# Two convolution layers with deformable sampling: hat loads in a running list, tails begun at the last unit that writes their rows, and the last tile row's branches reversed

## The chip, the cores and the metric

The kernel runs on 1 core of one Trainium2 chip. The metric is device time in microseconds (us) of one launch. The kernel before took 6643.4 us, the median of 3 runs (6639.72 to 6648.73).

## What is computed

The input x has shape (2, 256, 128, 128): two images of 256 channels and 128 x 128 pixels, in float32. Two layers are added to it in turn. Cut to what matters:

```python
x = x + layer0(group_norm(x))
x = x + conv3x3(group_norm(x), ternary_weights) + bias

def layer0(x):                                  # d = 1, 9, 12
    for d in dilations:
        off = conv3x3(x, w_off[d], dilation=d)  # 18 planes: (dy, dx) of 9 taps
        y = sum over 9 taps of w_def[c, tap] * bilinear(x, pixel + tap * d + off)
        x_d = gelu(channel_norm(y))
    out = channel_norm(x_1 + x_9 + x_12 + conv1x1(x))
    h = gelu(out @ w1 + b1) @ w2 + b2           # 256 -> 512 -> 256 per pixel
    return channel_norm(h + out)
```

## The kernel before

Three stages follow each other. The first computes moments and offsets and writes two things to DRAM: `tables`, x with the pixel as the row, and `hats`, the bilinear weights of each tap as two factors, one for the row and one for the column. The second, `sample_near` (L1257), samples and does the rest of layer 0. The third is the 3x3 convolution of layer 1. Between stages stands a branch that all engines pass.

Sampling goes by *units*, in the list `units` (L1262): image b, tile row Rt of 66 (two pixel rows each), branch br of 3 (dilations 1, 9, 12), in this order of nesting. A unit has up to three *taps* ky (L1310), those whose rows fall within the image. Near the top and the bottom of an image units have two taps or one: every unit of the first tile row and of the last has one, and branches 1 and 2 have two in many of the rows next to them.

For each tap `load_hats` (L1313) loads two tiles, hy and hx, of 288 KB each (half that where one row is valid), into three buffers of each name, from SP's queue. `build` (L1333) multiplies them on DVE into the matrix A, of which there are two, used in turn. `load_tiles` (L1291) loads the 11 xs tiles of a tile row, 96 KB each, into 18 buffers, also from SP's queue. `sample` (L1422 on) multiplies A with xs on PE for each of two halves of the channels, into four PSUM banks pm; ACT copies these to ev (L1460, L1468), of which there are three, and `accumulate` adds ev to the ring of the branch on DVE (L1409); the first tap of a new row is written by ACT (L1391). A ring holds 8, 24 or 32 rows of a branch. `prepare(u)` (L1477) builds all taps of unit u and then calls `load_hats(u + 1)`; unit u prepares unit u + 2 ahead of its second half's sums. After unit 1 `lacking` (L1498) does a block of DVE work on the few pixels that lie outside.

Four rows of a branch make a *group*, of which an image has 32. When its rows are complete a *tail* is begun for it (`branch`, L1156): it turns the rows (PE, tp), copies them (ACT), takes moments (DVE L1097 to L1102, POOL L1103 and L1104), scales and applies gelu (ACT L1111). Branch 0 stores the result in g12d, branch 1 loads that as `other`, adds it and stores the sum, and branch 2 loads the sum, adds it and goes on: the 1x1 convolution (PE, pc), norm, zc, the two layers of the MLP (PE hp L890 and h L1133), norm, zc, and the store in x1d. Tails are generators. `tail.begin` (L1504) queues one, first in, first out, ready 7 advances later (LAG), and with at least 2 advances (GAP) from one start to the next; `tail.advance` moves the running ones by a step. A unit of sampling advances them four times, and `accumulate` advances them as often as is needed before it writes a ring row whose old group has not been read yet (L1388). After the last unit a loop advances until all are done (L1508): the drain. The order of compute instructions is thus written out by hand (`pin`), and that of the DMAs on a queue follows a scheduler.

Which unit begins a group is worked out at L1264 to L1274: the first unit of the branch after which all rows of the group lie below what later tile rows reach, or the last tile row for what is left. `spot` (L1276) prepares the corrections of a branch 0 group on DVE and needs `count`, loaded at L1489.

Of the kernel before, what the change touches and what calls it, by code (L numbers as in the profile page):

```python
# [25 lines left out]
R = 4  # L26
NG = R * W
RC = 16
DILS = (1, 9, 12)
# [10 lines left out]
REACH = 2  # L40
RI, CI = 2, 12
TR, TC = RI + 2 * REACH, CI + 2 * REACH
NT = -(-(W + 2 * REACH) // CI)
# [7 lines left out]
BRS = (0, 1, 2)  # L51
# [20 lines left out]
def conv_preact_kernel(ctx: ExitStack, tc: tile.TileContext, t: dict, out: bass.AP):  # L72
    nc = tc.nc
    x = t["x"]
    NB, _, H, _ = x.shape
    HW = H * W
    NGRP = H // R
    NR = (H + 2 * REACH) // RI
# [629 lines left out]
    with ExitStack() as actx:  # L708
# [24 lines left out]
        for b in range(NB):  # L733
            stats = ap.tile([P, KC, NGRP, 6], F32, name=f"stats1_{b}", tag=f"stats1_{b}")
            for c in range(KC):
                for g0 in range(0, NGRP, XT):
                    xt = ap.tile([P, XT * NG], F32, name="xt", tag="xt", bufs=3)
# [97 lines left out]
    class Tail:  # L835
# [4 lines left out]
        def __init__(self, pool, psum, pin):  # L840
            self.pool, self.psum, self.pin = pool, psum, pin
            self.spots, self.extra = {}, None
            self.waiting, self.running = deque(), []
            self.now = self.last = self.norms = self.banks = 0
            self.read = set()

        def begin(self, chain, wait):
            self.waiting.append([self.now + wait, chain, 0, 1, False])
# [122 lines left out]
        def branch(self, b, br, g, y):  # L971

            pin = self.pin
            cols = slice(g * NG, (g + 1) * NG)
            gv = g12d[b].rearrange("(k p) f -> p k f", p=P)[:, :, cols]
            z = []
            yield from self.normalised(z, y, (b, br, g))
            v = z[0]
            for c in range(KC):
                pin(  # L980
                    nc.scalar.activation(
                        v[:, c, :], z[1 + c], AF.Gelu,
                        scale=bw[:, br, c : c + 1], bias=bb[:, br, c : c + 1],
                    )
                )
            if br == 0:
                yield 2
                nc.sync.dma_start(gv, v)
                return
            yield 1, 1 + br  # L990
            other = self.tile("other")
            nc.sync.dma_start(other, gv)
            if br == 1:
                yield 2
                pin(nc.vector.tensor_tensor(v, v, other, ALU.add))
                yield 2
                nc.sync.dma_start(gv, v)
                return
            xn = self.tile("xn")
            nc.sync.dma_start(xn, x[b].rearrange("(k p) h w -> p k (h w)", p=P)[:, :, cols])  # L1000
            yield 4
            for c in range(KC):
                pin(
                    nc.scalar.activation(
                        xn[:, c, :], xn[:, c, :], AF.Identity, bias=negmean[b][:, c : c + 1]
                    )
                )
            yield 1
            yield from self.finish(b, g, v, other, xn)
# [75 lines left out]
    class PixelTail(Tail):  # L1085
# [70 lines left out]
        def branch(self, b, br, g, y):  # L1156
# [16 lines left out]
            if br == 0:  # L1173
                yield 2
                nc.sync.dma_start(gv, vf)
                return
            other = self.tile("other")
            of = other.rearrange("p k n -> p (k n)")
            nc.sync.dma_start(of, gv)
            if br == 1:  # L1180
                yield 2
                pin(nc.vector.tensor_tensor(vf, vf, of, ALU.add))
                yield 2
                nc.sync.dma_start(gv, vf)
                return
            yield 1, 3
            xn = self.tile("xn")
# [69 lines left out]
    def sample_near(pool, psum, k):  # L1257
# [1 line left out]
        pin = tc.keep_in_program_order  # L1259
        count = pool.tile([P, NG], F32, name="count")  # L1260
        tail = PixelTail(pool, psum, pin)
        units = [(b, Rt, br) for b in range(NB) for Rt in range(NR) for br in BRS]  # L1262
        xts, hbs, owners, begun = {}, {}, {}, set()
        done = {(b, br): 0 for b in range(NB) for br in BRS}  # L1264
        begins, order = {}, []
        for u, (b, Rt, br) in enumerate(units):
            begins[u] = []
            while done[b, br] < NGRP and (
                Rt == NR - 1
                or (done[b, br] + 1) * R - 1 < (Rt + 1) * RI - REACH - DILS[br]  # L1270
            ):
                begins[u].append((b, br, done[b, br]))
                done[b, br] += 1
            order += [(wb, wg) for wb, wbr, wg in begins[u] if wbr == 0]  # L1274

        def spot(n):  # L1276

            if n >= len(order):
                return
            b, g = order[n]  # L1280
            S = pool.tile([P, NG], BF16, name="S", tag="S", bufs=5)
            if n >= 5:
                assert (order[n - 5][0], 2, order[n - 5][1]) in tail.read
            pin(
                nc.vector.tensor_scalar(
                    S, count, float((b * NGRP + g) * NG), ids, ALU.add, ALU.is_equal
                )
            )
            tail.spots[order[n]] = S

        def load_tiles(b, Rt):  # L1291

            xts[b, Rt] = []
            for T in range(NT):
                xt = pool.tile([PX, C], F32, name="xs", tag="xs", bufs=18)
                src = bass.AP(
                    table[b].tensor,
                    table[b].offset + (Rt * RI * WT + T * CI) * C,
                    [[C, TC], [WT * C, TR], [1, C]],
                )  # L1300
                nc.sync.dma_start(xt, src)
                xts[b, Rt].append(xt)

        def valid(Rt, br, ky):

            s0 = Rt * RI - REACH - ky * DILS[br]
            i0, i1 = max(0, -s0), min(RI, H - s0)
            return (i0, i1) if i0 < i1 else None

        def taps(u):  # L1310
            return [ky for ky in (-1, 0, 1) if valid(units[u][1], units[u][2], ky)]

        def load_hats(u):  # L1313
            b, Rt, br = units[u]
            for ky in taps(u):
                i0, i1 = valid(Rt, br, ky)
                hq = hats[b][br * 3 + ky + 1]
                y0 = Rt * RI - REACH - ky * DILS[br] + i0
                hy = pool.tile([PX, RI, 3, W], F32, name="hy", tag="hy", bufs=3)
                hx = pool.tile([PX, RI, 3, W], F32, name="hx", tag="hx", bufs=3)  # L1320
                pitch = HY * 3 * W
                for h, first, dims in (
                    (hy, 0, [[0, TC], [pitch, TR]]),
                    (hx, TR, [[pitch, TC], [0, TR]]),
                ):
                    src = hq[first, y0]
                    nc.sync.dma_start(
                        h[:, i0:i1].rearrange("p i t w -> p (i t w)"),
                        bass.AP(src.tensor, src.offset, dims + [[1, (i1 - i0) * 3 * W]]),
                    )  # L1330
                hbs[u, ky] = hy, hx

        def build(u, ky):  # L1333

            b, Rt, br = units[u]
            dil = DILS[br]
            i0, i1 = valid(Rt, br, ky)
            hy, hx = hbs.pop((u, ky))

            Af = k["A"][u % len(k["A"])].rearrange("p t i w -> p (t i w)")  # L1340
            dst = bass.AP(
                Af.tensor,
                Af.offset + ((ky + 1) * 3 * RI + i0) * WA + AO + REACH - dil,
                [list(Af.ap[0]), [RI * WA + dil, 3], [WA, i1 - i0], [1, W]],
            )
            pin(
                nc.vector.tensor_tensor(  # L1347
                    dst,
                    hy[:, i0:i1].rearrange("p i t w -> p t i w"),
                    hx[:, i0:i1].rearrange("p i t w -> p t i w"),  # L1350
                    ALU.mult,
                )
            )
# [123 lines left out]
        def prepare(u):  # L1477

            if u < len(units):
                for ky in taps(u):  # L1480
                    build(u, ky)
                if u + 1 < len(units):
                    load_hats(u + 1)

        load_hats(0)
        load_tiles(*units[0][0:2])
        prepare(0)
        prepare(1)
# [1 line left out]
        begun_groups = 0  # L1490
        spot(0)
        for u, (b, Rt, br) in enumerate(units):
            if br == BRS[0] and u + len(BRS) < len(units):
                load_tiles(*units[u + len(BRS)][0:2])
            for c in range(KC):
                sample(u, c)
            if u == 1:
                tail.extra = lacking(pool, tail.tile, miss, pin)  # L1498

            for what in begins[u]:  # L1500
                _, _, g = what
                r0 = g * R % RINGS[br]
                ring = k["rings"][br][:, :, r0 : r0 + R, :].rearrange("p k r w -> p k (r w)")
                tail.begin(tail.branch(b, br, g, ring), LAG)  # L1504
                if br == 0:
                    begun_groups += 1
                    spot(begun_groups)
# [462 lines left out]
```

## Time and profile before

| | |
|---|---|
| median of 3 runs | 6643.4 us |
| profiled execution | 6654.54 us |
| its span, first to last instruction | 6652.5 us |
| mean granted TensorE clock | 0.971 |
| busy: PE, PE weight loads, DVE, ACT, POOL | 6295.0, 5006.0, 5907.6, 4194.8, 687.1 us |
| first stage, sampling, last stage (from its windows) | 0 to about 916, to about 5858, to the end |
| chain that ended last: PE, DVE, DMA, ACT, issue | 54%, 28%, 8%, 6%, 3% |
| sampling matmuls, pm L1448 | 17424, 344 ns each |
| DVE waiting for hx at the build, L1347 | 100.2 us in 59 waits |

The page lists for every engine its busy time, the chain that ended last, groups of instructions by line, and DMA issues. Times within the execution count from the start of its span. PE is the matmul row, PEld its weight loads, which overlap it; SPq is SP's DMA queue. A matmul of float32 stands as two records. In brackets behind an instruction stands how long its engine was idle before it, and who ended that.

### The profile page before, as it was taken

How to read it: one execution, taken by the hardware profiler on the slowest of the kernel's cores; microseconds unless marked ns; L12 is line 12 of the kernel's file. 1: busy time of each engine (PE TensorE's matmuls, PEld its weight loads, DVE VectorE, ACT ScalarE, POOL GpSimd, SP SyncE). 2: the span in 40 equal slices, each digit the busy share in tenths (PEclk: the TensorE clock that was granted, in tenths of full speed). 3: DMA queues.
4: the chain of work that ended last, by engine and by line, in shares of the span. 5: the costliest groups of instructions: out<-in, count | busy, mean ns of one | idle time of the engine just before them, and what ended most of it. 6: DMA issues, size and time to landing. Idle time of an engine off the chain costs nothing.

```text
span 6652.5 us, 100588 instructions
## 1 busy us (share of the span) xinstructions
PE 6295.0 (95%) x32242; PEld 5006.0 (75%) x32242; DVE 5907.6 (89%) x13772; ACT 4194.8 (63%) x8690; POOL 687.1 (10%) x665
## 2 busy tenths in 40 slices
PE   5899978999999999999999999999999999989999
PEld 3455558888888888888888888888888888734444
DVE  7766657999999999999878999999999999689996
ACT  1344436677777777777676777777777777554442
POOL 0000000111111111111110111111111111200000
PEclk9999978999999999999999999999999999989999
DMA  8976657877887777877667877778777787343332
GB/s 285 281 211 196 201 158 208 227 220 218 222 224 217 219 215 222 226 220 210 189 192 199 226 221 218 216 221 229 224 217 220 218 222 207 121 163 132 135 141 90
DMA packets 635794, 1360.48 MB, mean 205 GB/s; under 512 B 109592, under 2 KB 290344, under 8 KB 618736
## 3 DMA queue, kind: packets, MB, share of 16 engines
q1 hardware_dynamic: 617328, 1318.97, 68.8%
q10 hardware_dynamic: 17408, 33.56, 1.6%
q8 instruction: 261, 4.28, 0.3%
q14 instruction: 285, 2.33, 0.1%
q0 software_dynamic: 512, 1.34, 0.1%
HBM read 1087.10 MB, written 266.47 MB: 203 GB/s over the span
## 4 chain that ended last, share of the span: by engine, by line
PE 54%; DVE 28%; DMA 8%; ACT 6%; issue 3%; SPq 1%; POOL 0%; DVEq 0%; ACTq 0%; POOLq 0%
PE pm L1448 23%; DVE ring L1409 12%; PE hp L890 6%; PE pc L1789 6%; PE h L1133 5%; PE pz L364 4%; DVE A L1347 4%; DMA hx<-hats 3%; ACT ev L1460 3%; PE pc L1133 2%; DMA xa<-in_x 2%; ACT v L1111 2%; PE ph L463 2%; PE tp L905 1%; DVE st L1097 1%
## 5 line engine op out<-in xcount | busy, mean ns | idle before, releaser
L1448 PE MATMUL pm<-A,xs 96*128 96x216 f32 (+2 forms) x17424 | 3258.3, 344 | 180.3 <-ACT ev L1460 44.4
L1448 PEld LDWEIGHTS pm<-A,xs 96*128 96x128 f32 x17424 | 3058.0, 195 | 380.0 <-ACT ev L1460 124.2
L1409 DVE SCALAR_TENSOR_TENSOR ring<-ev,defw,ring 128x256 f32<-128x256 f32 (+4 forms) x6372 | 2481.2, 451 | 98.1 <-ACT ev L1460 52.1
L1460 ACT COPY ev<-pm 128x432 f32<-128x432 f32 (+4 forms) x4488 | 1991.9, 483 | 883.2 <-PE pm L1448 702.4
L1347 DVE TENSOR_TENSOR A<-hy,hx 96x768 f32<-96x768 f32 (+1 forms) x1124 | 1010.3, 945 | 180.3 <-DMA hx<-hats 100.2
L1103 POOL TENSOR_TENSOR rs<-rs,mhalf 128x4 f32<-128x4 f32 x320 | 472.5, 1477 | 4223.5 <-DVE rs L1102 3672.0
L1789 PE MATMUL pc<-cring,signs 128*128 128x512 bf16 x3456 | 758.2, 383 | 17.0 <-ACT cring L1706 7.4
L1111 ACT ACTIVATE v<-v,rs 128x256 f32<-128x256 f32 x1280 | 694.2, 594 | 17.0 <-POOL rs L1104 16.8
L1789 PEld LDWEIGHTS <-signs 128*128 128x128 bf16 x3456 | 339.7, 98 | 434.8 <-issue 28.0
L890 PE MATMUL hp<-S,w 128*128 128x512 f32 x1024 | 500.5, 614 | 0.8 <-ACT S L1213 0.8
L364 PE MATMUL pz<-wz,xa 128*128 128x486 f32 x1024 | 463.5, 580 | 28.1 <-DVE zr L371 28.0
L1097 DVE BATCH_NORM_STATS2 st<-v 128x6 f32<-128x256 f32 x1280 | 446.9, 410 | 35.0 <-ACT v L921 35.0
L1133 PE MATMUL h<-w,hT 128*128 128x256 f32 x2048 | 477.1, 379 | 0.0
L1391 ACT ACTIVATE ring<-ev,defw 128x256 f32<-128x256 f32 (+1 forms) x856 | 404.4, 485 | 24.1
L1133 PEld LDWEIGHTS h<-w,hT 128*128 128x128 f32 x2048 | 369.3, 190 | 65.5 <-issue 1.0
L364 PEld LDWEIGHTS pz<-wz,xa 128*128 128x128 f32 x1024 | 189.5, 192 | 193.5 <-issue 126.8
L921 ACT COPY v<-tp 128x512 f32<-128x512 f32 x384 | 207.7, 597 | 183.5 <-PE tp L913 182.7
L1222 ACT ACTIVATE hT<-hp,b 128x512 f32<-128x512 f32 x256 | 176.1, 688 | 222.5 <-PE hp L890 217.3
L890 PEld LDWEIGHTS hp<-S,w 128*128 128x128 f32 x1024 | 198.8, 199 | 141.4 <-issue 126.8
L470 ACT ACTIVATE hb<-ph 96x512 f32<-96x512 f32 (+1 forms) x384 | 209.9, 596 | 145.0 <-PE ph L463 138.6
L1133 PE MATMUL pc<-convw,xn 128*128 128x256 f32 x1024 | 271.5, 394 | 2.5 <-ACT xn L1194 2.5
L371 ACT COPY zr<-pz 128x486 f32<-128x486 f32 x128 | 72.3, 565 | 260.0 <-PE pz L364 257.3
(246 smaller groups left out, 5135.7 us busy)
## 6 DMA issues: line engine op xcount, KB each, us to landing
hy<-hats SPq DMA_DIRECT2D x1112, 288.0 KB
hx<-hats SPq DMA_DIRECT2D x1112, 288.0 KB
xs<-tables SPq DMA_DIRECT2D x1452, 96.0 KB
g12d<-v SPq DMA_DIRECT2D x128, 512.0 KB
other<-g12d SPq DMA_DIRECT2D x128, 512.0 KB
hats<-hb SPq DMA_DIRECT2D x64, 720.0 KB
hats<-hb SPq DMA_DIRECT2D x64, 576.0 KB
xa<-in_x ACTq DMA_DIRECT2D x64, 512.0 KB
```

What stands on the lines that cost most here:

```text
L364: nc.tensor.matmul(pz[:, 0:NZ], lhsT=xt[:, c, r, :], rhs=k["wz"][:, c, :], start=c == 0, stop=c == KC - 1,)
L890: nc.tensor.matmul(out, lhsT=w, rhs=v, start=i == 0, stop=i == n - 1)
L1097: pin(nc.vector.bn_stats(st[:, j, :], rows[j]))
L1103: nc.gpsimd.tensor_tensor(rs[:, 0, :], rs[:, 0, :], mhalf[:, 0:n], ALU.pow)
L1111: nc.scalar.activation(row, row, func, scale=rs[:, 0, j : j + 1], bias=rs[:, 1, j : j + 1])
L1133: nc.tensor.matmul(bank[:, j, :], lhsT=v[:, px], rhs=w, start=False, stop=i == len(pairs) - 1,)
L1347: nc.vector.tensor_tensor(dst, hy[:, i0:i1].rearrange("p i t w -> p t i w"), hx[:, i0:i1].rearrange("p i t w -> p t i w"), ALU.mult,)
L1391: pin(nc.scalar.mul(dst, src, w))
L1409: pin(nc.vector.scalar_tensor_tensor(dst, src, w, dst, ALU.mult, ALU.add))
L1448: nc.tensor.matmul(pv[:, j, :, m0:m1, :], lhsT=xts[b, Rt][t][:, c * P : (c + 1) * P], rhs=A[:, y0:y1, m0:m1, AO + t * CI : AO + (t + 1) * CI],
L1460: nc.scalar.copy(dst.rearrange("p m (t j) -> p t m j", j=CI), pm[:, 0 : len(ts), 0:n].rearrange("p t (m j) -> p t m j", j=CI),)
L1789: nc.tensor.matmul(pc, lhsT=signs[:, k, (h * 3 + t) * 3 + kx, m * P : (m + 1) * P], rhs=xc[:, i, k, t * JC : (t + 1) * JC, kx : kx + W], s ...
```

## The change

- `load_hats` takes a place in a running list `items` of all (unit, tap) pairs. Three are loaded at first, and each build is followed by the load of the item three places on.
- The first 18 xs loads of image 0 go out on ACT's queue instead of SP's.
- `last` holds, for every group, the last unit that writes one of its rows; a group begins there, but not ahead of the group before it in its branch, nor ahead of the last unit that writes the same group of the branch before.
- In the last tile row of each image the branches run 2, 1, 0.
- A tail of branch 1 or 2 does not load `other` until the branch before it has issued its store of that group: it yields step by step.

```diff
-        units = [(b, Rt, br) for b in range(NB) for Rt in range(NR) for br in BRS]
+        units = [
+            (b, Rt, br)
+            for b in range(NB)
+            for Rt in range(NR)
+            for br in (BRS if Rt < NR - 1 else BRS[::-1])
+        ]
...
+        last = {}
         for u, (b, Rt, br) in enumerate(units):
-            begins[u] = []
-            while done[b, br] < NGRP and (
-                Rt == NR - 1
-                or (done[b, br] + 1) * R - 1 < (Rt + 1) * RI - REACH - DILS[br]
-            ):
-                begins[u].append((b, br, done[b, br]))
-                done[b, br] += 1
+            for ky in (-1, 0, 1):
+                if valid(Rt, br, ky):
+                    s0 = Rt * RI - REACH - ky * DILS[br]
+                    for y in range(*(s0 + i for i in valid(Rt, br, ky))):
+                        last[b, br, y // R] = u
+        begins, order = {u: [] for u in range(len(units))}, []
+        for b in range(NB):
+            for br in BRS:
+                at = 0
+                for g in range(NGRP):
+                    at = max(at, last[b, br, g])
+                    if br:
+                        at = max(at, last[b, br - 1, g])
+                    begins[at].append((b, br, g))
...
-                nc.sync.dma_start(xt, src)
+                (nc.scalar if b == 0 and Rt * NT + T < 18 else nc.sync).dma_start(xt, src)
...
-        def load_hats(u):
-            b, Rt, br = units[u]
-            for ky in taps(u):
+        def load_hats(i):
+            if i < len(items):
+                u, ky = items[i]
+                b, Rt, br = units[u]
...
                 for ky in taps(u):
                     build(u, ky)
-                if u + 1 < len(units):
-                    load_hats(u + 1)
-
-        load_hats(0)
+                    load_hats(items.index((u, ky)) + 3)
+
+        items = [(u, ky) for u in range(len(units)) for ky in taps(u)]
+        for i in range(3):
+            load_hats(i)
...
             if br == 0:
                 yield 2
                 nc.sync.dma_start(gv, vf)
+                self.stored.add((b, br, g))
                 return
             other = self.tile("other")
             of = other.rearrange("p k n -> p (k n)")
+            while (b, br - 1, g) not in self.stored:
+                yield 1
             nc.sync.dma_start(of, gv)
```

More of the change, by code (lines that the diff above doesn't have):

```diff
@@ L844, in __init__ @@
             self.now = self.last = self.norms = self.banks = 0
-            self.read = set()
+            self.read, self.stored = set(), set()
         def begin(self, chain, wait):
@@ L997, in branch @@
                 nc.sync.dma_start(gv, v)
+                self.stored.add((b, br, g))
                 return
@@ L1175, in branch @@
                 nc.sync.dma_start(gv, vf)
+                self.stored.add((b, br, g))
                 return
@@ L1178, in branch @@
             of = other.rearrange("p k n -> p (k n)")
+            while (b, br - 1, g) not in self.stored:
+                yield 1
             nc.sync.dma_start(of, gv)
@@ L1184, in branch @@
                 nc.sync.dma_start(gv, vf)
+                self.stored.add((b, br, g))
                 return
@@ L1261, in sample_near, with valid @@
         tail = PixelTail(pool, psum, pin)
-        units = [(b, Rt, br) for b in range(NB) for Rt in range(NR) for br in BRS]
-        xts, hbs, owners, begun = {}, {}, {}, set()
-        done = {(b, br): 0 for b in range(NB) for br in BRS}
-        begins, order = {}, []
-        for u, (b, Rt, br) in enumerate(units):
-            begins[u] = []
-            while done[b, br] < NGRP and (
-                Rt == NR - 1
-                or (done[b, br] + 1) * R - 1 < (Rt + 1) * RI - REACH - DILS[br]
-            ):
-                begins[u].append((b, br, done[b, br]))
-                done[b, br] += 1
+        units = [
[4 more added lines that the diff above has]
+        ]
+        xts, hbs, owners, begun = {}, {}, {}, set()
+        def valid(Rt, br, ky):
+            s0 = Rt * RI - REACH - ky * DILS[br]
+            i0, i1 = max(0, -s0), min(RI, H - s0)
+            return (i0, i1) if i0 < i1 else None
+        last = {}
+        for u, (b, Rt, br) in enumerate(units):
+            for ky in (-1, 0, 1):
+                if valid(Rt, br, ky):
+                    s0 = Rt * RI - REACH - ky * DILS[br]
+                    for y in range(*(s0 + i for i in valid(Rt, br, ky))):
[9 more added lines that the diff above has]
+                    begins[at].append((b, br, g))
+        for u in begins:
             order += [(wb, wg) for wb, wbr, wg in begins[u] if wbr == 0]
@@ L1300, in load_tiles @@
                 )
-                nc.sync.dma_start(xt, src)
+                (nc.scalar if b == 0 and Rt * NT + T < 18 else nc.sync).dma_start(xt, src)
                 xts[b, Rt].append(xt)
[L1304 to L1308, printed above, removed]
         def taps(u):
             return [ky for ky in (-1, 0, 1) if valid(units[u][1], units[u][2], ky)]
-        def load_hats(u):
-            b, Rt, br = units[u]
-            for ky in taps(u):
+        def load_hats(i):
+            if i < len(items):
+                u, ky = items[i]
+                b, Rt, br = units[u]
                 i0, i1 = valid(Rt, br, ky)
@@ L1492, in sample_near @@
         for u, (b, Rt, br) in enumerate(units):
-            if br == BRS[0] and u + len(BRS) < len(units):
+            if u % len(BRS) == 0 and u + len(BRS) < len(units):
                 load_tiles(*units[u + len(BRS)][0:2])
@@ L1498, in sample_near @@
                 tail.extra = lacking(pool, tail.tile, miss, pin)
-            for what in begins[u]:
-                _, _, g = what
+            for b, br, g in begins[u]:
                 r0 = g * R % RINGS[br]
```

## The prediction

> **What bounds the kernel now.** I read the busy times in 40 equal windows first, since the change touches only some stages. Columns: window and length, busy us (count) of PE, PEld, DVE, ACT and POOL, granted clock, DMA share, GB/s.
>
> ```profile
> 830.00:996.00 166.00, 117.81 (x555) 91.18 (x554) 97.81 (x283) 62.82 (x150) 16.22 (x14) 0.73 0.57 156
> ...
> 2490.00:2656.00 166.00, 162.97 (x857) 142.84 (x857) 159.51 (x408) 120.63 (x264) 22.33 (x22) 0.99 0.79 218
> ...
> 3320.00:3486.00 166.00, 157.42 (x898) 135.67 (x897) 125.01 (x326) 120.06 (x296) 21.41 (x26) 0.94 0.66 188
> ...
> 5810.00:5976.00 166.00, 134.85 (x583) 67.96 (x581) 133.44 (x228) 78.18 (x76) 4.33 (x7) 0.90 0.39 149
> ```
>
> In the middle of sampling PE is busy 98% and DVE 96%: nothing is to be had there. The start (830-996), the border between the images (around 3300) and the end of sampling (around 5850) have slack. Then the timelines of SP's queue and of DVE at the start of sampling:
>
> ```profile
> 917.28 6.99 SPq L1301 DMA_DIRECT2D xs<-tables  x11
> 924.31 0.59 SPq L1327 DMA_DIRECT2D hy<-hats  x1
> 924.95 0.59 SPq L1327 DMA_DIRECT2D hx<-hats  x1
> ...
> 926.87 1.50 SPq L1489 DMA_DIRECT2D count<-in_count  x1
> 928.42 8.34 SPq L1301 DMA_DIRECT2D xs<-tables  x7
> ...
> 950.52 2.85 SPq L1301 DMA_DIRECT2D xs<-tables  x4
> 953.47 0.54 SPq L1327 DMA_DIRECT2D hy<-hats  x1
> ```
> ```profile
> 959.01 1.66 DVE L1347 TENSOR_TENSOR A<-hy,hx 96x768 f32<-96x768 f32 x2 [12.61 <-DMA hx<-hats]
> ...
> 978.35 1.82 DVE L1347 TENSOR_TENSOR A<-hy,hx 96x768 f32<-96x768 f32 x2
> ...
> 999.08 0.96 DVE L1347 TENSOR_TENSOR A<-hy,hx 96x768 f32<-96x768 f32 x1 [2.87 <-DMA hx<-hats]
> ```
>
> The second pair of hats of unit 3 stands on SP behind four xs loads, which wait until 950.52 for PE to free their buffers; so the build at 959.01 is late, the long DVE job behind it (`lacking`, 961.66 to 977.4) too, and unit 4's builds come at 978.35. Last, PE's timeline of the drain after the last unit of image 1, where tails run alone:
>
> ```profile
> 5741.50 1.03 PE L1133 MATMUL pc<-convw,xn 128*128 128x256 f32 x4
> 5742.37 1.04 PE L905 MATMUL tp<-ident,ring 128*128 128x128 f32 x8
> ...
> 5755.29 5.48 PE L890 MATMUL hp<-S,w 128*128 128x512 f32 x8 [0.35 <-ACT S L1213]
> 5760.61 1.04 PE L905 MATMUL tp<-ident,ring 128*128 128x128 f32 x8
> 5761.48 0.60 PE L913 MATMUL tp<-extra,S 128*128 128x256 bf16 x4
> 5761.92 1.88 PE L890 MATMUL hp<-S,w 128*128 128x512 f32 x4
> ...
> 5781.14 0.33 PE L1150 MATMUL zc<-ident,v 128*128 128x128 f32 x1 [1.75 <-ACT v L1111]
> ...
> 5785.20 2.07 PE L1133 MATMUL pc<-convw,xn 128*128 128x256 f32 x4 [1.16 <-ACT xn L1194]
> ```
>
> From 5742.4 to 5755.3 PE has 4.5 us of work (two tp groups, two zc groups) in 12.9; the eight hp behind it take 685 ns each, later ones 430. A tail is a chain through ACT, DVE, POOL and ACT again; without sampling between its links PE waits for them.
>
> **What the Trainium skill says.** "DMA: Bandwidth & Descriptors", section "Issuing engines are not separate DMA queues": transfers begun on several engines share the same 16 DMA engines, and only the issuer's time is saved. The trace agrees as far as it can: at 936-948 the 16 engines move 128 GB/s at a share of 0.44, at 996-1008 247 at 0.97; so ACT's queue saves the 11 x 0.64 us that SP spends, not bandwidth. "TensorE: Matmul & The Clock Gate", section "What's actually happening": an idle PE falls to half clock after some 3.4 us and needs as long busy to come back. The drain shows it (685 against 430 ns), so a hole costs some 2 us beyond its length.
>
> **The change, part by part.** I compared the order of instructions on every engine in both built programs. The order differs at the start (SP and ACT only, to about tile row 6), at the image border and at the end; everything between is the same, so it costs nothing.
>
> *Hats, in the loop: 0.* A load already waits only for its own buffer: the hx/hy pair issued at 1000.06 follows the build that ended at 1000.04, three builds earlier in the list. Three in flight is what three buffers gave. Only places on SP's queue change.
>
> *Hats and xs at the start: -13.* Now six hats loads lead (6 x 0.6 = 3.7 us), the 18 xs go to ACT. I price an xs issue on ACT as on SP, 0.64 us (ACT's own xa issue took 0.37): 18 x 0.64 = 11.5 us in front of ACT's first eviction, which moves from 920.8 to 927.5. Behind it wait the four pm banks and so PE: 14 of unit 0's 44 matmuls fit in them, the other 30 at 0.216 us end at 934, where before they ended at 934.9, since tiles arrived slowly. So that is free; if ACT's issue were twice as slow, it would cost 8. Count is issued at about 926 as before, so unit 2 ends near 955 as before (954.8). The gain: unit 3's second hats follow the build of unit 1, near 926 instead of 953.5, so its builds stand at 945-949 instead of 960.6, `lacking` starts near 950 and ends near 967, and unit 4's builds come at 968 instead of 978.35: -10. Rows 2 to 6: DVE waits 20-odd us there for hats, but the four xs loads stand between the same hats as before, so I take -3 (0 to -8). Together -13, ends -4 and -20.
>
> *Reversed branches and begins at the image border: +8.* Tail begins of an image's end come in this order now: branch 1 groups 29, 30; branch 2 groups 29, 30, 31 (after the second unit of the last row), branch 0 group 31, branch 1 group 31 (after the last). Each starts at least 2 advances after the one before, so branch 1 group 31 is seventh, not fourth. Image 1's second unit writes ring rows that it owns (L1388), so sampling must push the tails until it has been read. In the built program PE gets five tp, three zc, a whole hp and h and a pc group in a row, with no sampling between: the same sequence as the drain above. Price from there: 12.9 - 4.5 + 2 = 10 us for the first hole; 5779.2 to 5785.2 less 0.9 of zc, plus 2.5 for slow pc, = 8 for the second. +18. Against it: before loses about 10 us at 3322-3349 (26.6 us for 16 of PE work: slow clock, waits for evictions) around the same units, of which I take half back, and the hats waits after the border (3306 to 3346 and 3486) give 5. +8; ends -5 (the holes are filled by work I count as done) and +20 (nothing comes back).
>
> *SP's queue at the border: 0.* The run's stores and loads (four g12d stores, six loads of `other`, xn, xr, two x1d stores) now stand ahead of the hats of image 1's unit 4. Those are built at the end of its unit 2, one and a half units after the run ends, some 10 us at 72 columns; a load takes about 4 (955.34 to 960.0). If that cover is missing, 4 us.
>
> *Stored waits: 0.* They are in the program's making, not on the chip; a waiting tail holds two v buffers and lets others pass. Group 31 hands over branch 0 to 1 to 2 through DRAM: about 32 us from branch 0's tp to branch 2's sum, while PE has 36 of other tails. If that cover is missing, up to 5.
>
> *The end: +4.* Same work, five tails, one tp group moved behind the last sampling matmul and one in front less: 0. First two holes as before. But the last tail's hp stands behind group 30's last zc, which must wait for its moments: from the drain, h's end to zc's last is 5775.3 to 5783.8 = 8.5 us, then S; PE has 2.8: hole 6.2 + 2 = 8. Back comes 3.4 (5841.2 to 5844.6, other groups' sums ahead of the last moments on DVE), which now lie earlier. +4 to +5; ends -4 and +12.
>
> Sum: -13 + 8 + 4 = -1 against the profiled execution's 6654.5 us (span 6652.5 and 2.0 around it), which lies 11.1 above the median of the runs, 6643.4. So 6642.
>
> **Rivals.** *Faster:* the border run is hidden, since ACT and DVE are not behind there, and the start gives its full end: -20 + 0 + 0 = -20: 6623. For it: DVE is busy 75% there, and PE loses clock anyway. Against: L1388 leaves PE nothing else in program order. *Slower:* one mechanism, tails run alone at the border: 20 with nothing back, +12 at the end by the same holes, -12 at the start: +20: 6663. It decides as soon as the holes exceed what the start gives, 13. For it: the drain's holes are measured. Against: before has a slow patch there too. *The list does nothing:* as worked out, in the loop it can't; were the start not helped either (ACT's issue slow), 6655, inside the range.
>
> **How the numbers follow.** Forecast case, within 0.2% (13 us, about what a measurement of this kernel can tell from no change): 0.43, from 6630 to 6656. Faster, 0.35; slower, 0.22. The range reaches 6616 to 6664, nearly to both rivals' times.
>
> **What would show it.** Right: unit 4's builds near 968; no hats wait of 12 us on DVE; around 3322-3375 some 40 us without a pm matmul and two holes on PE; one hole before the last hp; equal times between 1200 and 3250. Wrong: PE standing before 927 for evictions longer than before; rows 1 to 6 taking 10 us less; sampling matmuls inside the border run.

## The result and the profile after

| | before | after |
|---|---|---|
| median | 6645.3 us (6 runs) | 6678.7 us (6 runs) |
| ratio, 95% interval | 1 | 1.0046 [1.0033, 1.006] |
| profiled execution, span | 6654.5, 6652.5 us | 6674.4, 6672.5 us |
| busy PE, DVE, ACT | 6295.0, 5907.6, 4194.8 us | 6310.5, 5908.0, 4191.7 us |
| mean granted clock | 0.971 | 0.970 |

The change costs time: the medians lie 33 us apart, and the ratio, 0.46%, is 31 us. I forecast no difference (6642), in a range up to 6664: wrong, and on the far side of the slower rival.

First the same four windows as before, now of the changed kernel (columns: window and length, busy us and count of PE, PEld, DVE, ACT and POOL, granted clock, DMA share, GB/s):

```profile
830.00:996.00 166.00, 125.24 (x592) 97.53 (x591) 101.35 (x289) 69.24 (x163) 16.57 (x14) 0.74 0.62 168
2490.00:2656.00 166.00, 163.09 (x859) 143.73 (x858) 159.69 (x413) 118.36 (x260) 24.96 (x25) 0.99 0.80 223
3320.00:3486.00 166.00, 150.71 (x799) 120.86 (x798) 106.93 (x273) 105.90 (x250) 19.22 (x25) 0.93 0.53 155
5810.00:5976.00 166.00, 137.93 (x578) 72.87 (x577) 118.15 (x211) 75.71 (x82) 5.78 (x11) 0.89 0.36 136
```

The start got more done (592 matmul records for 555), the middle is as it was, the border got less done (799 for 898, DVE 107 us for 125).

To find where the time goes I counted sampling matmuls (pm) in both traces: there are 17424 records in each, and they do the same work until the last tile row. Record 1290 comes 12.9 us earlier than before and record 8436 13.6 earlier; record 8815, just behind the border, comes 50.2 later, record 9928 12.3 later. By the last one the difference is +2.4, and by the end +20. The 10 us between record 9928 and the last one lie in a stretch that no edit touches and are within its own spread (below). So there are three places:

- *start*: from the first memset of pm, with which the sampling stage begins, to record 1290;
- *border*: from record 8350 to record 9934, which takes in the last tile row of image 0 and the first ones of image 1;
- *drain*: from the last pm to the first matmul of the next norm (gnps).

From here on these three stand for each kernel. They repeat better than the whole time: single executions of one kernel lie up to 28 us from its median, and stretches that no edit touches move too (from record 9934 to the last: 2078 to 2096 us over all the runs, the start of the sampling stage: 907 to 926).

**The start.** ACT's queue and ACT, then the durations of the xs issues (ns, shortest, median and longest), then PE, then DVE, of after:

```profile
915.94 19.42 ACTq L1328 DMA_DIRECT2D xs<-tables  x18
935.40 0.77 ACT L1482 COPY ev<-pm 128x72 f32<-128x72 f32 x4 [25.65 <-DMA xs<-tables]
```
```profile
L1328 ACTq DMA_DIRECT2D xs<-tables x18: 548/607/810, 915.9 to 934.8; - x18
```
```profile
927.93 0.70 PE L1470 MATMUL pm<-A,xs 96*128 96x72 f32 x2 [1.01 <-DMA xs<-tables]
935.67 4.54 PE L1470 MATMUL pm<-A,xs 96*128 96x72 f32 x20 [7.04 <-issue]
```
```profile
943.77 0.48 DVE L1312 TENSOR_SCALAR S<-count,ids 128x512 bf16<-128x512 f32 x1 [16.82 <-DMA count<-in_count]
...
970.88 0.96 DVE L1431 SCALAR_TENSOR_TENSOR ring<-ev,defw,ring 128x236 f32<-128x236 f32 x2
971.75 1.81 DVE L1369 TENSOR_TENSOR A<-hy,hx 96x768 f32<-96x768 f32 x2
```

The 18 xs loads take ACT 19.42 us, one every 1.08 us where SP issued one every 0.64. An issue itself is no dearer on ACT: 0.61 us at the median, and 0.60 for each of SP's first eleven in before. The other 8.6 us lie between the issues, from the sixth on: they wait, and the trace puts the end of the two longest waits (2.65 and 1.44 us) down to hats loads of SP. The DMA engines are full in that time; in before, while SP's first eleven went out, they were not (the last two columns are DMA share and GB/s). After, then before:

```profile
921.00:936.00 15.00, 4.41 (x16) 3.61 (x16) 1.58 (x2) 0.60 (x4) 10.11 (x11) 0.50 1.03 249
```
```profile
918.00:927.00 9.00, 4.71 (x16) 3.89 (x16) 0.56 (x1) 1.06 (x4) 7.36 (x6) 0.50 0.69 175
```

The first eviction stands behind all 18, and PE, its four banks full, stands for 7 us until 935.67. On SP `count` goes out at 936.25, nine us later than before, and DVE waits 16.8 us for it; PE has no gap from 935.67 to 970.66, so this wait costs nothing that shows. Still, unit 4's builds come at 971.75 in place of 978.35, since the hats of unit 3 no longer stand behind xs loads that wait for PE. DVE's waits, before and after:

```profile
DVE A L1347 <- DMA hx<-hats: 100.2, 59, 12.9
```
```profile
DVE A L1369 <- DMA hx<-hats: 61.6, 54, 6.2
```

**The border.** PE's timeline of before, where sampling comes back 11 us after the first half of image 1's second unit:

```profile
3313.74 1.46 PE L1448 MATMUL pm<-A,xs 96*128 96x72 f32 x12
...
3324.54 1.14 PE L905 MATMUL tp<-ident,ring 128*128 128x128 f32 x8 [0.46 <-ACT v L921]
3325.52 0.60 PE L913 MATMUL tp<-extra,S 128*128 128x256 bf16 x4
3325.95 1.68 PE L1448 MATMUL pm<-A,xs 96*128 96x72 f32 x14
```

and of after:

```profile
3310.91 1.46 PE L1470 MATMUL pm<-A,xs 96*128 96x72 f32 x12
...
3322.70 0.33 PE L1154 MATMUL zc<-ident,v 128*128 128x128 f32 x1 [1.44 <-ACT v L1115]
...
3328.86 2.81 PE L1154 MATMUL zc<-ident,v 128*128 128x128 f32 x8 [2.62 <-ACT v L1115]
3331.79 5.67 PE L890 MATMUL hp<-S,w 128*128 128x512 f32 x8
...
3357.33 2.80 PE L1154 MATMUL zc<-ident,v 128*128 128x128 f32 x8 [6.46 <-ACT v L1115]
3359.92 0.42 PE L1133 MATMUL pc<-row,ones 128*128 128x256 bf16 x1
3361.38 2.08 PE L1137 MATMUL pc<-convw,xn 128*128 128x256 f32 x4 [1.04 <-ACT xn L1202]
...
3369.09 1.68 PE L1470 MATMUL pm<-A,xs 96*128 96x72 f32 x14
```

From 3312 to 3369 there is no sampling: tails run alone, and PE waits 1.4, 2.6, 6.5 and 1.0 us for ACT, which is the last link of each tail's chain through ACT, DVE and POOL. In the stretch PE is idle 32.3 us, where kernels with the old order have 21.0 to 23.7.

**The drain**, PE's timeline of after:

```profile
5783.94 2.80 PE L1154 MATMUL zc<-ident,v 128*128 128x128 f32 x8 [6.46 <-ACT v L1115]
...
5799.56 1.83 PE L1137 MATMUL pc<-convw,xn 128*128 128x256 f32 x4 [2.80 <-ACT xn L1202]
...
5845.56 2.81 PE L1154 MATMUL zc<-ident,v 128*128 128x128 f32 x8 [3.04 <-ACT v L1115]
5848.15 8.65 PE L890 MATMUL hp<-S,w 128*128 128x512 f32 x16
...
5868.94 2.80 PE L1154 MATMUL zc<-ident,v 128*128 128x128 f32 x8 [4.78 <-ACT v L1115]
5879.96 0.56 PE L191 MATMUL gnps<-gnmv,gmask 128*128 128x2 f32 x2 [8.21 <-DVE gnmv L187]
```

The last tail's whole second half, from hp at 5848 on, stands alone at the end. Before, three tails ended together:

```profile
5840.94 1.91 PE L1150 MATMUL zc<-ident,v 128*128 128x128 f32 x16
5848.65 2.80 PE L1150 MATMUL zc<-ident,v 128*128 128x128 f32 x8 [5.79 <-ACT v L1111]
```

### The profile page after: what moved, and what is told of

Same layout as the page of the kernel before. It is cut to its first block, busy times and chain, and to the rows that moved or that the text cites. A ratio compares the mean times of both kernels' runs of the same rounds, so it can differ in the third digit from the quotient of the medians.

```text
span 6672.5 us, 100590 instructions
## 1 busy us (share of the span) xinstructions
PE 6310.5 (95%) x32242; PEld 5014.9 (75%) x32242; DVE 5908.0 (89%) x13772; ACT 4191.7 (63%) x8690; POOL 689.4 (10%) x665
```

## The experiments

Theory A: three costs that add up: the start gains, the border loses by the run of tails, the drain loses because the chain of group 31 (branch 0 to 1 to 2 through DRAM) starts with the tail that begins last. The rivals are named in each expectation. All three stretches in us, from one traced execution of each kernel; time, over all its executions, as ratio to the kernel before in the same comparison:

| kernel | start | border | drain | time, 95% interval |
|---|---|---|---|---|
| before | 305.3 | 420.1 | 138.2 | 1 |
| after | 292.1 | 446.0 | 156.1 | 1.0046 [1.0033, 1.006] |
| e1_start | 294.7 | 415.2 | 137.4 | 1.0001 [0.9992, 1.0011] |
| e2_order | 298.2 | 435.6 | 156.0 | 1.0065 [1.0046, 1.0083] |
| e3_border | 294.6 | 445.5 | 138.6 | 1.0015 [1.0007, 1.0023] |
| e4_end | 293.4 | 416.5 | 155.7 | 1.002 [1.0012, 1.0028] |
| e5_fifo | 294.1 | 436.5 | 156.8 | 1.0066 [1.0049, 1.0082] |
| e6_nohand | 291.6 | 445.0 | 147.8 | one execution |
| e6_head | 297.3 | 434.1 | 144.6 | one execution |
| e7_list | 294.5 | 419.1 | 137.9 | 0.9982 [0.9972, 0.9991] |
| e8_xsact | 296.8 | 421.0 | 137.8 | 0.9974 [0.9951, 0.9996] |
| e9_tails | 297.0 | 438.9 | 156.1 | 1.0042 [1.003, 1.0055] |
| e10_head | 292.5 | 423.7 | 144.0 | 1.0015 [1.0006, 1.0024] |
| e11_b2last | 290.5 | 426.0 | 144.9 | 1.0015 [1.0002, 1.0028] |
| e12_both | 291.9 | 418.4 | 137.4 | 0.999 [0.9978, 1.0001] |
| e13_list | 288.1 | 416.5 | 137.9 | 0.9983 [0.9974, 0.9993] |
| e14_xsact | 294.9 | 412.9 | 137.5 | 0.9985 [0.9975, 0.9995] |

Means: start 301.8 with the loads of before (two kernels) and 293.6 with list and ACT (eleven), -8; border 417.5 with the old order (eight) and 441.2 with that of the change (five), +24; drain 138 and 156, +18. Sum +34; measured 31 to 33. The border's 24 holds some 6 us that come from the clock in three of the five executions (last section).

The start of the old loads is known from two executions only. It shows more plainly in two other things: the wait for unit 3's second hats, 12.6 and 11.8 us, is in those two kernels and in none of the other fifteen, and unit 4's first build comes 62.7 and 60.3 us after the first memset there, 53.6 to 57.9 in the others.

### Halves and places

**e1_start**, the start alone:

```diff
-            for br in (BRS if Rt < NR - 1 else BRS[::-1])
+            for br in BRS
```

> The change with the branches of the last tile row in the old order (0, 1, 2); the running list of hats and the 18 xs loads on ACT stay. With that order the new rule for the begins gives the same begins as before, so only the start differs. Theory A (the start gains what the trace of after shows at 1200 to 3200 us, 13 us, and keeps it to the end): 13 to 14 us below before, about 6632. Rival B (what the start gains is lost again at the first place where something else is late, the border or the drain): within 3 us of before.

Measured 1.0001, where A's 8 us (not the 13 I wrote) would be 0.9988: just outside its interval, and for rival B. In its trace the start's gain is there (294.7, and no wait for unit 3's hats), but its whole time says little, since that execution was the fastest of 14, 24 us below their median. e12 to e14 take this up.

**e2_order**, the rest alone: in the changed kernel `load_hats` is that of before again, and all xs go out on SP.

```diff
-                (nc.scalar if b == 0 and Rt * NT + T < 18 else nc.sync).dma_start(xt, src)
+                nc.sync.dma_start(xt, src)
...
-                    load_hats(items.index((u, ky)) + 3)
+                if u + 1 < len(units):
+                    load_hats(u + 1)
```

> The other half alone: branches reversed in the last tile row, new begins and stored waits, but hats and xs loaded as before. Theory A (the reversal costs 16 to 29 us at the border between the images and 18 in the drain): 34 to 47 us above before, 6679 to 6692. Rival B (the start is worth nothing in the end): as far above before as the whole change was, 33 us, 6678.

1.0065 is 43 us, as A has it; but the interval, 31 to 55 us, holds B's 33 too, so this run doesn't decide between them. Its start, 298.2 us with the very loads of before, where before's profile has 305.3, tells how far one execution's start can be trusted: to some 7 us.

**e3_border** and **e4_end**, the reversal in one image only:

```diff
-            for br in (BRS if Rt < NR - 1 else BRS[::-1])
+            for br in (BRS[::-1] if Rt == NR - 1 and b == 0 else BRS)
```

(b == 1 in e4_end.)

> The change with the reversal only in image 0, so that its start and the border are those of the change and the drain is that of before. Theory A (the border's holes on PE are lost for good): 13 us gained at the start, 16 to 29 lost at the border, so 3 to 16 above before, 6648 to 6661. Rival C (image 1's sampling makes the border good; only the drain costs): as the start alone, 6632.

> The change with the reversal only in image 1: start and drain of the change, border of before. Theory A (the drain costs 18, since branch 0 of the last group is the head of its chain and now begins last): 4 us above before, about 6649; the drain from the last sampling matmul to the first matmul of the next stage's norm takes 156 us in place of 138. Rival D (the drain's length hides behind the next stage's start): as the start alone, 6632.

Each shows one of the two stretches lengthened and the other as before; both are slower than before, by 10 and 13 us. Rivals C and D fall: neither place is hidden. (e3_border's traced execution, with 445.5 us at the border, was the longest of its 22, 15.6 us above their median.)

### What makes the border dear

**e5_fifo**:

```diff
-                    if br:
+                    if br == 2:
                         at = max(at, last[b, br - 1, g])
```

> The changed kernel with one clause of the begins taken out for branch 1: its group 31 begins with its own last unit, not with branch 0's. The queue of an image's end is then branch 1 groups 29, 30, 31, branch 2 groups 29, 30, 31 and last branch 0 group 31, and the ring rows that image 1's second unit needs are free third, not seventh. Theory A (at the border the cost is the run of tails that sampling must push until branch 1 group 31 is read): no run without sampling matmuls at the border, and the stretch from matmul 8436 to matmul 9913 takes 392 to 400 us as with the old order, not 412 to 422; at the end the head of group 31's chain, branch 0, now begins last of all, so the drain takes over 156 us. Rival E (the border pays for the order of sampling, or for tails that are simply late): 412 or more at the border. Time by A: 24 less than the change and the longer drain, 6655 to 6665.

A fell here as I had put it. From record 8436 to 9913 it takes 412.9 us, as in the change (410.6 to 422.3), not 392 to 400. The run at the second unit of image 1 is gone, but another stands behind record 8998, in the first half of image 1's unit of tile row 2, branch 0. That unit writes row 4, and in a ring of 8 rows row 4 lies where group 31 of image 0 lay, whose tail I had put last. It has an idle gap of 6.3 us, and a second, shorter run, behind record 9162, one of 6.6. So the wait was moved, not removed. In the drain the hole that I had expected is there, since branch 2 now waits for the whole chain:

```profile
5785.02 0.42 PE L1133 MATMUL pc<-row,ones 128*128 128x256 bf16 x1
5799.66 2.07 PE L1137 MATMUL pc<-convw,xn 128*128 128x256 f32 x4 [14.21 <-ACT xn L1202]
```

but the drain as a whole is no longer than the change's, against my number, since the last three tails end together behind that hole. Its time, 1.0066 or 44 us, is above what its stretches add up to (-8 + 19 + 19 = 30), though the traced execution was the fastest of four, 21 us below their median; that stays open.

**e9_tails** and **e10_head** separate the order of sampling from the order of the tails. e9 samples in the old order with the change's tails, e10 samples reversed with the tails of before. In e9 (the first line also as in e1):

```diff
+        for n in (197, 395):
+            end = [w for u in (n - 2, n - 1, n) for w in begins[u]]
+            begins[n - 2], begins[n - 1] = [], []
+            begins[n] = [end[i] for i in (1, 2, 4, 5, 6, 0, 3)]
```

and in e10

```diff
+            begins[n - 2], begins[n - 1], begins[n] = [], [], sorted(end)
```

> Sampling in the old order of branches, but the seven tails of each image's end in the order of the change (branch 1 groups 29, 30, branch 2 groups 29 to 31, branch 0 group 31, branch 1 group 31), all begun after the last unit, since the rows are complete only there. Start as in the change. PE's order at the border is then the change's: five turned groups, three zc, hp, h and pc in a row without sampling. Theory A (order of the tails, and what image 1's second unit must wait for, makes the border dear): from matmul 8350 to matmul 9934 432 to 446 us, with idle gaps of about 1.5, 2.6, 6.5 and 1 us in the run; drain 150 or more. Rival E (the order of sampling is what costs): 415 to 421 at the border, drain 138 to 142.

> The counterpart: sampling reversed, but the seven tails of each image's end begun after its last unit in the order of before (branch 0 group 31, then branch 1, then branch 2). The ring rows that image 1's second unit needs are then read by the fourth tail, and no tail gets past its first half before. Theory A: from matmul 8350 to matmul 9934 416 to 426 us, without a gap over 2 us before a zc; drain 144 to 146 as in the run with that order in image 1 alone. Rival E: 432 or more at the border.

e9: 438.9 at the border and 156.1 in the drain, as the change, though the sampling is that of before. Its gaps are the change's:

```profile
3333.82 0.33 PE L1154 MATMUL zc<-ident,v 128*128 128x128 f32 x1 [2.51 <-ACT v L1115]
...
3336.75 5.79 PE L890 MATMUL hp<-S,w 128*128 128x512 f32 x8
...
3362.41 2.81 PE L1154 MATMUL zc<-ident,v 128*128 128x128 f32 x8 [6.46 <-ACT v L1115]
```

e10: 423.7 at the border, with sampling back after 20 us of tails; one gap before a zc is 3.4 us, more than I had written:

```profile
3326.89 0.33 PE L1154 MATMUL zc<-ident,v 128*128 128x128 f32 x1 [3.40 <-ACT v L1115]
...
3331.71 1.90 PE L1473 MATMUL pm<-A,xs 96*128 96x72 f32 x14
```

So the order of the tails makes most of the border's cost, by when the tails are read that ring rows wait for: 15 us from e9 to e10, and 11 from e10 to the two executions of the change without the clock's extra 9 us of the last section (e2_order and e6_head, 435.6 and 434.1), which lie 17 above the old order. The rest, some 6 us in e10, comes with the reversed sampling or with the later begins; no run parts these two. Rival E falls as the main cause.

**e11_b2last**, the repair that keeps the reversal:

```diff
+            end = [w for u in (n - 1, n) for w in begins[u]]
+            begins[n - 1] = [w for w in begins[n - 1] if w[1] == 1]
+            begins[n] = sorted(w for w in end if w not in begins[n - 1])
```

> The changed kernel with branch 2's last three tails put behind: branch 1 groups 29 and 30 begin after the last but one unit, then branch 0 group 31, branch 1 group 31 and branch 2 groups 29 to 31 after the last. Theory A (what matters is how early the tails stand that others wait for: branch 1 group 31 for the ring, branch 0 group 31 for the chain): 415 to 426 us at the border, drain 140 to 146, in time 20 to 30 us below the change. Rival E: border as in the change, 432 or more.

426.0, 144.9 and 1.0015, about 20 us below the change and still above before. A holds.

### What makes the drain long

**e6_nohand**: branches 1 and 2 of group 31 of image 1 load group 0's sum and wait for nobody.

```diff
-            while (b, br - 1, g) not in self.stored:
+            own = (b, g) != (1, NGRP - 1)
+            while own and (b, br - 1, g) not in self.stored:
                 yield 1
-            nc.sync.dma_start(of, gv)
+            nc.sync.dma_start(of, gv if own else g0)
```

> The changed kernel, in which the tails of group 31 of image 1 don't wait for one another: branches 1 and 2 add what stands in group 0's place of g12d, long stored, in place of their own group's partial sum; the count of instructions and loads stays. So this kernel computes a wrong sum in that group. Theory A (the drain is long because the chain of three tails through DRAM starts with the one that begins last): the drain, from the last sampling matmul to the first matmul of the next norm, falls from 156 us to 138 to 147. Rival F (the drain is long because PE's order has holes between whatever tails stand there): 152 or more.

**e6_head**: image 1's last tails in the order of before, all after its last unit (the edit of e10 for 395 alone).

> The changed kernel with image 1's last seven tails begun together after its last unit in the order of before: branch 0 group 31 first, then branch 1 groups 29 to 31, then branch 2. The sampling order stays reversed. Theory A (order of the tails, not of sampling, makes the drain long): 136 to 144 us. Rival F (the reversal of sampling itself makes it long, as more tails are left behind the last matmul): 150 or more.

147.8 and 144.6: each just past my bound, but far below 152. So the chain behind a head that begins last costs 8 us (156.1 - 147.8), the order as a whole 11 to 12. The last 6 to 7 us stay even in e10 (144.0 against 138). I put them down to the reversal itself: the head of the chain can't begin before the last unit when that unit writes its rows. This is argued; no run shows it apart. F falls as the whole cause and may hold for this third.

### What the start gains, and what a better kernel is

**e7_list**: e1_start with all xs on SP. **e8_xsact**: the kernel before with the ACT line alone.

> The running list of hats alone: all xs on SP, branches in the old order. On SP six hats then lead, the 11 xs of the first tile row follow, the hats of unit 2, count, seven xs, and the four xs that wait for PE stand behind unit 3's first hats. Theory A (what the start gains comes from hats ahead of waiting xs loads; ACT's 1.08 us per xs in front of its first eviction takes back part): matmul 1290 comes 284 to 292 us after the stage's first memset of pm, against 292 to 295 in the runs with xs on ACT and 298 to 305 with the loads of before. Rival G (moving the xs to ACT is what gains): 298 or more.

> The kernel before with only the first 18 xs loads of image 0 on ACT's queue. With these gone from SP, the hats of unit 3 stand there ahead of the four xs loads that wait for PE, without any list. Theory A (hats ahead of waiting xs loads are the whole gain at the start, whichever edit brings it): matmul 1290 at 291 to 297 us after the stage's first memset of pm, as in the runs with list and ACT together. Rival H (the list's three builds ahead are needed): 298 to 305 as before.

Starts of 294.5 and 296.8 (288.1 and 294.9 when run again, below), unit 4's first build 54.9 and 56.6 us after the first memset: either edit alone brings the gain. With the xs gone from SP, or with the list, the scheduler puts unit 3's second hats before or well clear of the xs loads that wait for PE. Rivals G and H fall. Since e1 with both had shown nothing in time, I ran all three side by side:

> The list and the xs on ACT together, branches in the old order, measured again beside each of the two alone. Theory A (all three have the same start and nothing else differs): the same ratio for the three, 8 us below before, 0.9988, and matmul 1290 at 291 to 297 us after the first memset of pm. Rival K (the two together cost something later that the traces don't show): 1.000 here, and below 0.999 for each alone.

> The list alone again. Theory A: 0.9988 as for both together. Rival K: 0.998, and above that for both together.

> The xs on ACT alone again. Theory A: 0.9988 as for both together. Rival K: 0.998, and above that for both together.

0.999, 0.9983 and 0.9985, all overlapping, as A has it. K isn't excluded: its 1.000 lies in the first interval too, and e1, the same kernel, had 1.0001. Whether the two together cost something stays open; no stretch shows it. That the gain reaches the end is shown for each alone: the list, with the branches in the old order, was 0.9982 and 0.9983 in two comparisons, the xs on ACT 0.9974 and 0.9985, all four intervals below 1. The list alone is some 11 us under before and 42 to 44 under the change. Either is a kernel to keep; the runs don't part them.

## Why the prediction was wrong, point by point

- *Hats in the loop, 0:* right. From record 1290 to 8436 before takes 2010.8 us and after 2010.0.
- *Start, -13:* right in mechanism, 8 in size. Unit 4's builds came at 971.75, not 968. I had priced the issues on ACT (0.64 us, and they took that) and not their waits: the 18 took 19.4 us in place of 11.5, so that the first eviction came at 935.4, not 927.5. I had named the case of a slower ACT and its cost. But this explains little of the shortfall: with the xs on SP, e7 and e13 have unit 4's first build 54.9 and 53.6 us after the first memset, the eleven with list and ACT 54.3 to 57.9. The rest stays open. "Count is issued at about 926 as before" was wrong too (936.25), at no cost that shows.
- *Border, +8:* this step failed. The holes were right: I wrote 18 for both with their slow clock. The run has 11.6 us of gaps, its first hp at 709 ns and pc at up to 1.9 us per group in place of 450 and 1.0, and e2_order and e6_head, whose clock ahead of the run was that of before, lie 17 us above the old order. What failed is "I take half back" and the hats waits: the 10 us that were to come back. None did. DVE's waits for hats in the stretch did shrink, from 23.1 us to 12.1, but PE gained nothing by it: means of five and eight kernels, it is idle 33.5 us for 22.0 and busy 407.7 for 395.5; both differences are costs, and there is no gain beside them. The half clock makes nearly all of the busy time's 12 us: 58 us of PE's busy time lie in it in place of 36, which at half speed is 11. Some 6 of the 24, the half clock ahead of the run in three of the five executions, was not in my sum at all.
- *The end, +4:* right in kind, 18 in size. "First two holes as before" failed: the second grew to 6.5 us, one of 2.8 and one of 3.0 came anew, and the hole that I had put before the last hp is not there; instead the last hp and h run alone. PE is idle 10.3 us longer, has 12 tp records more to do (1.5 us, which I had put at 0), and loses 6 more in half clock. I priced the hole of the last tail, and not that its whole second half would stand alone behind the chain. Of the 3.4 that were to come back 1.0 did: the last zc waits 4.8 us in place of 5.8.
- *SP's queue, 0:* no run shows a cost of it there.
- *Stored waits, 0:* failed in the drain, which is 8.3 us shorter without those of group 31 (e6_nohand), more than the 5 that I had put for a missing cover. "Group 31 hands over in 32 us, while PE has 36 of other tails" didn't hold for the tail at the end.
- *The slower rival* had the mechanism (tails alone at the border, nothing back) and 6663. It missed the drain's size (12 for 18) and had 12 for 8 at the start, and I gave it 0.22 since I counted on time coming back that I had not traced to an instruction.

## What to carry to other kernels

When tails wait for each other or hold buffers, look at which one others wait for and begin that one first; a new order of the work that leaves the head of a chain last pays at each end of the loop. A stretch where the filler work is gone costs its holes and the clock behind them, and nothing of it comes back unless you can name the instruction that was waiting for something else. A load that needn't wait belongs ahead of loads that must, on the queue where it stands; that alone was the gain here, by either of two edits.

## What the runs showed of the hardware

The Trainium skill, "TensorE: Matmul & The Clock Gate", section "What's actually happening", has the half clock follow an idle window of some 3.4 us. The traces show it without one. In after, ahead of the border's run, PE is busy by the trace for the whole of 38.5 us (records 8614 to 8746) and has the half clock for most of it:

```profile
3262.13:3300.66 38.53, 38.53 (x173) 34.30 (x174) 18.42 (x55) 16.77 (x52) 3.70 (x4) 0.58 0.46 140
```

In e2_order the same instructions had

```profile
3271.94:3301.15 29.21, 29.21 (x173) 26.00 (x174) 18.41 (x56) 15.96 (x52) 4.57 (x4) 0.78 0.42 128
```

that is 9 us less for the same work. After, e3_border and e6_nohand took the long way (37.9 to 38.7 us), the fourteen others the short one (26.4 to 30.6). One of these is e6_head, whose order is the change's until the end of image 1, so the execution differs there and not the program. This is most of what parts 445 from 435 at the border. Whether the 72 columns of those matmuls have to do with it no run tested, and why one execution takes the one way and another the other stays open. The drain of before, which I had read as agreeing with the page, has no idle gap over 2.3 us ahead of its half clock at 5748.7 either.

A 96 KB xs load took about 0.6 us to issue on ACT's queue as on SP's. What set the pace of the 18 on ACT, one every 1.08 us, was the waits between them, while the DMA engines moved 249 GB/s at a share of 1.03.
